# A cross-attention's query map folded into the context side, in a kernel of an RWKV block and an attention

## The chip, the cores and the metric

The kernel runs on one core of a Trainium2 chip. The metric is the device time of one execution in microseconds (us), and lower is better. The engines of the core run side by side and wait for each other by semaphores: TensorE (PE, matrix products into the PSUM memory), VectorE (DVE), ScalarE (ACT), GpSimd (POOL) and SyncE (SP), which here only issues DMAs. Work that one engine is given runs in the order in which it was put in that engine's queue.

## What is computed

Two layers run over 16 sequences of 128 tokens with 512 channels, in float32. The first is an RWKV block (layer norm, token mixing by small matrices, six large projections, a recurrence over time, a group norm and a feed-forward part). The second is a cross-attention between its result, `x_c`, and a context `x_s`. There the roles of the axes differ: the 128 tokens are the channels C, and the 512 channels are the positions T.

```python
def _inorm(x):                                   # over the last axis
    return (x - mean(x)) * rsqrt(var(x) + EPS)

Mn = einsum('oc,bct->bot', Wn, _inorm(x_c)) + bn     # queries
Mm = einsum('oc,bct->bot', Wm, _inorm(x_s)) + bm     # keys
A  = softmax(einsum('bct,bcs->bts', Mn, Mm), axis=-1)
Ml = einsum('oc,bct->bot', Wl, x_s) + bl             # values
Mo = einsum('bcs,bts->bct', Ml, A)
return einsum('oc,bct->bot', Wo, Mo) + bo + x_c
```

All of Wn, Wm, Wl and Wo are 128 x 128. For each of the 16 sequences the scores are a 512 x 512 matrix, and the softmax runs along its rows.

## The kernel before

The 16 sequences are worked in G = 8 groups of n = 2. Each group passes through stages, written as Python generators: `stageB` and `stageB2` (first norm, token mixing, projections), `stageR` (the recurrence), `stageC` (output projection, second norm, feed-forward part), `stageX` (loads the prepared context of the group) and `stageL` (the cross-attention, by `stageLb` for each of the two sequences). `stageE` prepares the contexts of all groups, by `context`, in the first three steps. In each step `interleave` takes pieces of the stages of different groups in turn, in an order given by `ORDER`, `DLY` and the numbers of pieces in `ST`; `NEED` says which stage of a group must be finished first. The framework's scheduler then fixes the order of every engine's queue before the run, and puts in the waits. Tiles come from pools: tiles with one tag share a fixed number of buffers, and a new tile waits until the old one of its slot is no longer read.

The weights' projections are plain matmuls: one float32 matmul is recorded as two passes on PE. All loads and stores are issued by SP, whose queue is in order too.

What the change touches:

- `load_late` (L86) loads the small constants, among them `bdm` (a mask of 128 x 8 x 16) and `emat` (a 0/1 matrix: partition p belongs to column p // 16), and the attention's weights in two loads, `wnm` (Wn and Wm) and `lo` (Wl and Wo). It multiplies Wl and Wo on PE once (`pc`), so that the values already carry the output map.
- `context` (L640) loads one context, normalises its rows (`inorm`, L635, on DVE, POOL and ACT), multiplies by Wm and adds bm on the way out of PSUM (`pm`, L649 and L650), makes the values (`pV`, L654 and L655) and writes both, 128 x 1024, to a DRAM tile `mvD` (L657). `stageX` loads it again as `MV`, just ahead of use (`MVl` for the last group).
- `stageLb` (L680) normalises the rows of x (`xh`), multiplies by Wn (`pn`, L687), adds bn on ACT (`Mn`, L689), and then works four tiles of 128 query positions. For each: scores `pS` (L693) on PE, the negated row maximum (L695) on DVE, exponential and row sum (L697) on ACT, reciprocal (L698) on DVE, scaling (L699) on ACT, four transposes into `pA` (L702) on PE and a copy to `AT` (L705) on ACT. After each two tiles the product with the values, `pO` (L711), is added to x (L713).
- In `stageR`, `spread` (L476) and the operation at L481 place states of the recurrence block by block into `Sx`, by a multiplication with `bdm`.

PSUM has eight banks, shared out by tags: `bx`, `c` and `lv` have two buffers each, `ls` and `la` one each. `pc`, `pm`, `pn` and `pS` use `ls`; `pV`, `pA` and `pO` use `la`. The last group takes others instead, where they are free by then. In SBUF the tag `e` has two buffers.

## Time and profile before

| | |
|---|---|
| runs, us | 993.84, 993.47, 990.04; median 993.47 |
| profiled execution, us | 989.27 |
| its span in the profile, us | 987.5 |
| busy PE, DVE, ACT, POOL, us | 903.8, 638.4, 502.4, 59.6 |
| mean clock granted to PE | 0.977 of full speed |

The profile is of one execution. The span runs from the first to the last instruction that it shows. Busy times are of the engines' instructions; as matmuls are pipelined, the recorded duration of a PE pass is longer than the time after which the next can follow. "PEld" are loads of the stationary operand of a matmul, which overlap with PE. Groups of instructions are listed with the line, engine and operation, the tile written, "<-" and the tiles read, their shape, the count, busy time in us and mean duration in ns, and after the bar the engine's idle time just before them, with what ended it. The chain of work that ended last is followed back from the last instruction, at each step to what released it. A number such as L687 is a line of the kernel before.

### The profile page before, as it was taken

How to read it: one execution, taken by the hardware profiler on the slowest of the kernel's cores; microseconds unless marked ns; L12 is line 12 of the kernel's file. 1: busy time of each engine (PE TensorE's matmuls, PEld its weight loads, DVE VectorE, ACT ScalarE, POOL GpSimd, SP SyncE). 2: the span in 40 equal slices, each digit the busy share in tenths (PEclk: the TensorE clock that was granted, in tenths of full speed). 3: DMA queues.
4: the chain of work that ended last, by engine and by line, in shares of the span. 5: the costliest groups of instructions: out<-in, count | busy, mean ns of one | idle time of the engine just before them, and what ended most of it. 6: DMA issues, size and time to landing. Idle time of an engine off the chain costs nothing.

```text
span 987.5 us, 19150 instructions
## 1 busy us (share of the span) xinstructions
PE 903.8 (92%) x7524; PEld 614.0 (62%) x7524; DVE 638.4 (65%) x1573; ACT 502.4 (51%) x1053; POOL 59.6 (6%) x92
## 2 busy tenths in 40 slices
PE   4889998899989999999999999999999979988966
PEld 3666767666745767486757676767657645654534
DVE  5786678945695849766877587846944587354131
ACT  4675273442464545644556456534552566367243
POOL 5120010001000100000001000000000000000000
PEclk9999999998999999999999999999999999999987
DMA  6575756355414444363436334543445322431300
GB/s 197 188 266 188 207 166 223 75 153 202 141 43 116 153 152 139 75 212 103 129 110 172 128 117 122 141 148 99 142 107 159 100 97 66 149 108 53 96 0 21
DMA packets 76603, 129.90 MB, mean 132 GB/s; under 512 B 33713, under 2 KB 43697, under 8 KB 76512
## 3 DMA queue, kind: packets, MB, share of 16 engines
q1 hardware_dynamic: 76514, 128.68, 42.4%
q8 instruction: 59, 0.97, 0.4%
q14 instruction: 30, 0.25, 0.1%
HBM read 100.32 MB, written 22.04 MB: 124 GB/s over the span
## 4 chain that ended last, share of the span: by engine, by line
PE 60%; DVE 19%; ACT 8%; DMA 6%; SPq 4%; issue 2%; POOL 1%; ACTq 0%; DVEq 0%; POOLq 0%
PE ptk L581 14%; PE pj L224 8%; PE pj L608 6%; PE pv L331 6%; PE pO L711 4%; PE pS L693 4%; PE pl L446 3%; DVE PP L384 3%; PE pA L702 2%; SPq L415 2%; DVE xm L289 2%; PE po L522 2%; DVE xm L290 1%; PE pa L515 1%; PE pu L494 1%
## 5 line engine op out<-in xcount | busy, mean ns | idle before, releaser
L224 PE MATMUL pj<-xm,wb 128*128 128x256 f32 x768 | 175.8, 381 | 2.1 <-DMA wb<-in_Wg_dram 1.4
L224 PEld LDWEIGHTS pj<-xm,wb 128*128 128x128 f32 x768 | 142.8, 190 | 27.2 <-issue 5.9
L143 POOL TENSOR_TENSOR rs<-rs,mhalf 128x1 f32<-128x1 f32 x64 | 41.5, 653 | 656.7 <-DVE rs L128 575.7
L693 PE MATMUL pS<-MV,Mn 128*128 128x512 f32 x112 | 59.8, 616 | 5.9 <-ACT e L697 5.2
L697 ACT ACTIVATE e<-pS,nm 128x512 f32<-128x512 f32 x64 | 44.4, 694 | 39.8 <-DVE nm L695 39.4
L695 DVE TENSOR_REDUCE nm<-pS 128x1 f32<-128x512 f32 x64 | 43.8, 687 | 30.4 <-PE pS L693 30.2
L608 PE MATMUL pj<-xk,wb 128*128 128x256 f32 x256 | 62.1, 396 | 0.2 <-DVE xk L150 0.2
L711 PE MATMUL pO<-AT,MV 128*128 128x256 f32 x224 | 58.4, 400 | 2.9 <-ACT AT L705 2.9
L331 PE MATMUL pv<-wb,xm 128*128 128x512 f32 x128 | 58.9, 610 | 1.4 <-DVE xm L289 1.4
L699 ACT ACTIVATE e<-e,nm 128x512 f32<-128x512 f32 x64 | 46.1, 725 | 27.1 <-DVE nm L698 27.0
L581 PE MATMUL ptk<-wb,sx 128*128 128x512 f32 x128 | 58.0, 597 | 1.4 <-ACT kk L611 1.4
L581 PE MATMUL ptk<-wb,kk 128*128 128x512 f32 x128 | 58.4, 596 | 0.2
L289 DVE TENSOR_TENSOR xm<-px,sx 128x512 f32<-128x512 f32 x80 | 53.6, 684 | 6.6 <-PE px L286 6.6
L581 PE MATMUL ptk<-wb,yT 128*128 128x512 f32 x128 | 57.2, 597 | 0.2
L608 PEld LDWEIGHTS pj<-xk,wb 128*128 128x128 f32 x256 | 49.9, 199 | 9.1 <-issue 1.0
L290 DVE TENSOR_TENSOR xm<-xm,xaT 128x512 f32<-128x512 f32 x80 | 54.3, 687 | 0.3
L702 PEld LDWEIGHTS pA<-ident,e 128*128 128x128 f32 x256 | 30.6, 143 | 35.1 <-issue 14.7
L713 DVE SCALAR_TENSOR_TENSOR x<-pO,cb,x 128x256 f32<-128x256 f32 x32 | 15.4, 480 | 55.9 <-PE pO L711 55.9
L702 PE MATMUL pA<-ident,e 128*128 128x128 f32 x256 | 41.1, 282 | 11.2 <-ACT e L699 7.5
L711 PEld LDWEIGHTS pO<-AT,MV 128*128 128x128 f32 x224 | 42.4, 196 | 14.0 <-issue 4.6
L705 ACT COPY AT<-pA 128x512 f32<-128x512 f32 x64 | 37.4, 584 | 24.0 <-PE pA L702 23.6
L286 PE MATMUL px<-sk,w2s 98*128 98x256 f32 x160 | 42.0, 357 | 7.7 <-DVE gt L345 2.7
(162 smaller groups left out, 1680.8 us busy)
## 6 DMA issues: line engine op xcount, KB each, us to landing
wb<-in_Wk_dram SPq DMA_DIRECT2D x16, 512.0 KB, 4.7
mvD<-MVe SPq DMA_DIRECT2D x16, 512.0 KB, 2.9
wb<-in_Wr_dram SPq DMA_DIRECT2D x16, 512.0 KB, 3.5
wb<-wvc SPq DMA_DIRECT2D x16, 512.0 KB, 3.4
wb<-in_Wg_dram SPq DMA_DIRECT2D x16, 512.0 KB, 3.5
wb<-in_Wo_dram SPq DMA_DIRECT2D x16, 512.0 KB, 3.6
wb<-in_Wfk_dram SPq DMA_DIRECT2D x16, 512.0 KB, 4.0
wb<-in_Wfr_dram SPq DMA_DIRECT2D x16, 512.0 KB, 3.9
```

What stands on the lines that cost most here:

```text
L224: nc.tensor.matmul(pj[:, m], lhsT=wb[:, m, cc, :], rhs=xm[:, cc], start=cc == 0, stop=cc == 3)
L289: nc.vector.tensor_tensor(xm[:, sl], px.rearrange("p c (b t) -> p c b t", b=n), sx[:, sl], ALU.mult)
L290: nc.vector.tensor_tensor(xm[:, sl], xm[:, sl], xaT[:, sl, :, 1:129], ALU.add)
L331: nc.tensor.matmul(pv, lhsT=xm[:, m, b], rhs=wbs[m // 2][:, m % 2], start=m == 0, stop=m == 3)
L581: nc.tensor.matmul(pt, lhsT=act[:, m, b], rhs=wbs[m // 2][:, m % 2], start=m == 0, stop=m == 3)
L608: nc.tensor.matmul(pj[:, m], lhsT=wb[:, m, cc, :], rhs=xk2[:, cc], start=cc == 0, stop=cc == 3)
L693: nc.tensor.matmul(pS, lhsT=Mn[:, tsl], rhs=Mm, start=True, stop=True)
L695: nc.vector.tensor_reduce(nm[:, 0:1], pS, AX.X, ALU.max, negate=True)
L697: nc.scalar.activation(e, pS, AF.Exp, bias=nm[:, 0:1], accum_out=nm[:, 1:2])
L699: nc.scalar.activation(e, e, AF.Identity, scale=nm[:, 2:3])
L702: nc.tensor.transpose(pA[:, sc], e[:, 128 * sc : 128 * sc + 128], ident)
L711: nc.tensor.matmul(pO, lhsT=Vc[:, sc], rhs=AT[:, sc], start=sc == 0, stop=sc == 3)
```

## The change

With h the normalised rows of x and g those of the context, the scores are (Wn h + bn)ᵀ(Wm g + bm). The part hᵀ Wnᵀ bm is kept with hᵀ(Wnᵀ Wm) g, and the parts that do not depend on h, bnᵀ Wm g + bnᵀ bm, form one bias for each column. So the change makes Wmᵀ Wn once in `load_late`, multiplies g by it in `context` instead of by Wm, with q0 = Wnᵀ bm as bias, and takes h itself as the stationary operand of the score matmul. `pn`, `Mn` and the map by Wn are gone from `stageLb`.

The column bias is made in `context` by a further matmul of four 32-column pieces, `pb`, which uses the `la` bank; ACT takes it to SBUF (`bt`, in the buffer of `AT`) with bnᵀ bm added, and it is written to a DRAM tile of 512 values, `btD`. `stageX` loads it, copied to all 128 partitions, as `BB` (`BBl` for the last group). In `stageLb` one DVE operation, `tensor_tensor_reduce`, adds the bias to the scores out of PSUM, negates, writes the result to `e` and gives its minimum along the row. The exponential then reads `e` instead of `pS`, with scale -1.

To make room in SBUF, `bdm` is dropped and `emat`, read with a broadcast innermost axis, takes its place, and `var`, `gv`, `gt` and `gr` have one buffer instead of two. The attention's weights come in one load. `xh` has two buffers instead of one.

```diff
-    td1, td2, l1b, emat, bdm, lvm, dgm = late.values()
-    wnm = const.tile([128, 2, 128], FP, name="wnm")
-    WnT, WmT = wnm[:, 0], wnm[:, 1]
+    td1, td2, l1b, emat, lvm, dgm = late.values()
+    wq = const.tile([128, 162], FP, name="wq")
+    wqT, q0, vk, kk0 = wq[:, 0:128], wq[:, 128:129], wq[:, 129:161], wq[:, 161:162]
...
-        nc.sync.dma_start(out=wnm, in_=a["l1w"][:, 0:2])
-        lo = sb.tile([128, 2, 128], FP, name="lo", tag="e", bufs=2)
-        nc.sync.dma_start(out=lo, in_=a["l1w"][:, 2:4])
-        Wl, WoT = lo[:, 0], lo[:, 1]
+        l1w = sb.tile([128, 4, 128], FP, name="l1w", tag="e", bufs=2)
+        nc.sync.dma_start(out=l1w, in_=a["l1w"])
+        Wn, Wm, Wl, WoT = (l1w[:, i, :] for i in range(4))
...
+        bnr = sb.tile([128, 128], FP, name="bnr", tag="e", bufs=2)
+        nc.vector.tensor_scalar(bnr, ident, 0.0, l1b[:, 0:1], ALU.mult, ALU.add)
+        pq = pc[:, 129:291]
+        nc.tensor.matmul(pq[:, 0:128], lhsT=Wm, rhs=Wn, start=True, stop=True)
+        nc.tensor.matmul(pq[:, 128:129], lhsT=Wn, rhs=l1b[:, 1:2], start=True, stop=True)
+        nc.tensor.matmul(pq[:, 129:161], lhsT=Wm, rhs=bnr[:, 0:32], start=True, stop=True)
+        nc.tensor.matmul(pq[:, 161:162], lhsT=bnr, rhs=l1b[:, 1:2], start=True, stop=True)
+        nc.vector.tensor_copy(wq, pq)
...
-        var = small.tile([128, n, 32], FP, name="var", bufs=2)
+        var = small.tile([128, n, 32], FP, name="var", bufs=1)
...
-                o = Sx[:, c].rearrange("p m (a q) j -> p m a (q j)", a=2)
-                nc.vector.tensor_tensor(o, src, bdm.rearrange("p (a q) j -> p a (q j)", a=2)[:, None].to_broadcast([128, 4, 2, 64]), ALU.mult)
+                o = Sx[:, c].rearrange("p m (a q) j -> p m a q j", a=2)
+                own = emat[:, 0:8].rearrange("p (a q) -> p a q", a=2)[:, None, :, :, None].to_broadcast([128, 4, 2, 4, 16])
+                nc.vector.tensor_tensor(o, src, own, ALU.mult)
...
-    def inorm(xap, tag, how, ssum=None, tile_=dict(tag="l1n", bufs=1)):
+    def inorm(xap, tag, how, ssum=None, tile_=dict(tag="l1n", bufs=2)):
...
+        pb = ps.tile([128, 128], FP, name="pb", **T("la"))
+        for sc in range(4):
+            nc.tensor.matmul(pb[32 * sc : 32 * sc + 32], lhsT=vk, rhs=xsn[:, 128 * sc : 128 * sc + 128], start=True, stop=True)
+        bt = sb1.tile([128, 128], FP, name="bt", tag="AT")
+        nc.scalar.activation(bt, pb, AF.Identity, bias=kk0)
+        btD = dr.tile([1, 512], FP, name="btD", bufs=16)
+        nc.sync.dma_start(out=btD.rearrange("o (c s) -> (o c) s", c=4), in_=bt[0:128:32])
         pm = ps.tile([128, 512], FP, name="pm", **T("ls"))
-        nc.tensor.matmul(pm, lhsT=WmT, rhs=xsn, start=True, stop=True)
-        nc.scalar.activation(mv[:, 0:512], pm, AF.Identity, bias=l1b[:, 1:2])
+        nc.tensor.matmul(pm, lhsT=wqT, rhs=xsn, start=True, stop=True)
+        nc.scalar.activation(mv[:, 0:512], pm, AF.Identity, bias=q0)
...
             with behind(g + 2):
-                nc.sync.dma_start(out=mv, in_=d["mvD"][b])
-            d["MV"].append(mv)
+                nc.sync.dma_start(out=mv, in_=d["mvD"][b][0])
+                nc.sync.dma_start(out=bb, in_=d["mvD"][b][1].to_broadcast([128, 512]))
+            d["MV"].append((mv, bb))
...
         xh = inorm(xb, "xh", "act", d["ssum"][b])
-        pn = ps.tile([128, 512], FP, name="pn", **T("ls", g, ("lv", "bx")[b]))
-        nc.tensor.matmul(pn, lhsT=WnT, rhs=xh, start=True, stop=True)
-        Mn = sb.tile([128, 512], FP, name="Mn")
-        nc.scalar.activation(Mn, pn, AF.Identity, bias=l1b[:, 0:1])
         for tt in range(4):
             tsl = slice(128 * tt, 128 * tt + 128)
             pS = ps.tile([128, 512], FP, name="pS", **T("ls", g, ("c", "lv")[b]))
-            nc.tensor.matmul(pS, lhsT=Mn[:, tsl], rhs=Mm, start=True, stop=True)
+            nc.tensor.matmul(pS, lhsT=xh[:, tsl], rhs=Qm, start=True, stop=True)
             nm = small.tile([128, 3], FP, name="nm")
-            nc.vector.tensor_reduce(nm[:, 0:1], pS, AX.X, ALU.max, negate=True)
             e = sb.tile([128, 512], FP, name="e")
-            nc.scalar.activation(e, pS, AF.Exp, bias=nm[:, 0:1], accum_out=nm[:, 1:2])
+
+            nc.vector.tensor_tensor_reduce(e, pS, bb, -1.0, 3.4e38, ALU.add, ALU.min, nm[:, 0:1])
+            nc.scalar.activation(e, e, AF.Exp, bias=nm[:, 0:1], scale=-1.0, accum_out=nm[:, 1:2])
```

`WnT` and the like are transposed on the host before, and `Wn` and `Wm` are passed as they are after. The load of `bdm` and its preparation on the host are gone as well.

## The prediction

> **What bounds the kernel now.** I read the page's busy shares first, then its slices, then busy time by stage, because a share over the whole span mixes stages with different limits.
>
> ```profile
> PE 903.8 (92%) x7524; PEld 614.0 (62%) x7524; DVE 638.4 (65%) x1573; ACT 502.4 (51%) x1053; POOL 59.6 (6%) x92
> ...
> PEclk9999999998999999999999999999999999999987
> ```
>
> TensorE (PE) is busy for 92% of the span at an almost full clock; ScalarE (ACT) for half. By stage (stretch, PE, weight loads, VectorE (DVE), ACT, GpSimd, clock, DMA):
>
> ```profile
> 15.00:143.00 128.00, 116.93 (x868) 85.69 (x869) 97.73 (x274) 74.77 (x158) 19.09 (x27) 0.99 0.63 204
> ...
> 400.00:700.00 300.00, 297.64 (x2660) 208.00 (x2659) 210.58 (x504) 158.58 (x342) 10.01 (x20) 1.00 0.44 133
> ...
> 880.00:988.00 108.00, 81.31 (x354) 47.40 (x351) 31.86 (x86) 48.49 (x96) 2.19 (x4) 0.88 0.12 39
> ```
>
> From 400 to 700 us PE idles 2.4 us in 300: matmul time removed there is time gained. Up to 143 us, where the contexts are prepared, PE idles 9%, and in the last 108 us 25% (the last groups' attention, one step after another). The chain of work that ended last agrees: PE 60%, DVE 19%. The groups of the attention, by shape (line, engine, operation, count, busy us, mean ns, idle before and its releaser):
>
> ```profile
> L687 PE MATMUL pn<-l1n,wnm 128*128 128x512 f32 x32 | 18.1, 650 | 8.4 <-ACT e L697 5.0 <-ACT l1n L145 3.4
> L689 ACT ACTIVATE Mn<-pn,l1b 128x512 f32<-128x512 f32 x16 | 11.0, 687 | 6.9 <-PE pn L687 6.8
> L693 PE MATMUL pS<-MV,Mn 128*128 128x512 f32 x112 | 59.8, 616 | 5.9 <-ACT e L697 5.2 <-ACT Mn L689 0.6
> L695 DVE TENSOR_REDUCE nm<-pS 128x1 f32<-128x512 f32 x64 | 43.8, 687 | 30.4 <-PE pS L693 30.2
> L697 ACT ACTIVATE e<-pS,nm 128x512 f32<-128x512 f32 x64 | 44.4, 694 | 39.8 <-DVE nm L695 39.4
> ```
>
> The query map is 16 float32 matmuls in 32 passes; before them PE idles 8.4 us, mostly until an exponential frees the one-buffer "ls" bank. A mean of 650 ns is no price, since passes overlap. The chain lists 16 passes of the same width (ptk) in 7.07 us: 0.44 us each.
>
> **The change part by part.**
>
> Query map gone. 32 x 0.43 us (6.87 us for 16 in an undisturbed piece of the chain) = -13.7 us of PE. 16 bias activations of 0.687 us = -11.0 us of ACT, which does not set the pace; they count only in the tail, below.
>
> "ls" freed earlier. The bank is now released by DVE, not by the exponential after it (0.69 us and its queue). Idle for that reason: 5.0 us at pn, 5.2 us at pS. Bounds: 0 (the static order finds another wait) and -10.2; I take -4, since in 400 to 700 us only 0.2 us of such a wait was seen, and elsewhere PE often meets another wait next (xh, the normalised rows, 3.4 us at pn now).
>
> Tail. The last group's first score tile waits today from 944.39 (pn starts) to 946.29 (pS starts): pn 1.14, Mn 0.70. The other half has pn on the chain for 1.71. Sum 3.6, of which 1.7 (four passes) is already counted: -1.9.
>
> Per-context bias (stage E), PE. pb is four 128x32 matmuls in four column groups, 8 passes. L446 has exactly this shape: 64 passes in 1.89 us, 0.03 each, since four groups run side by side. 16 x 8 x 0.03 = +3.8. If they did not share the array, pV's price holds (8 passes in 1.16 us, 0.145): +18.6. I take 3.8, the identical shape.
>
> Per-context bias, waits. pb takes the one-buffer "la" bank that only pV used here. pV needs just xs and today often runs while xs is normalised (at 21.52, before pm at 22.52); it must now share the bank with pb, which needs the normalised rows and an ACT evacuation (128x128 out of PSUM: L303, 0.284). Queued behind a waiting pV on PE: the projections; behind pV's end: the next xs load, on the SP queue (it waits for pV 7.3 us in all today). Bounds: 0 where PE finds the bank free, and about 1.6 us per context (pb 0.24, bt 0.28, and one ACT queue of the kind seen at 24.74, where pV's copy stood behind 4 us of casts) = +26. I take 0.25 us per context, +4, near the evacuation alone, because today's pV idles PE 3.2 us over 16 contexts (L654), 0.2 each, on the same bank. bt lies in the single AT buffer until its write has been read out (the mvD writes land in 2.9 us); 16 contexts in 118 us come some 7 us apart: 0, and where two come close ACT waits up to 2.9 us, with mv's copies behind it.
>
> DVE's fused operation. 64 reductions of 0.687 are replaced by 64 operations that also read bb and write e. Nearest rows: scalar_tensor_tensor with an accumulator, one input in PSUM (L586, 689 ns + an 83 ns read, which overlaps its end) and two float32 SBUF inputs (L628, 690 + 83). So +0.09 x 64 = +5.5 us of DVE at most; at DVE's 19% of the chain, +1. Bounds from both sides: 0, and 1.22 us each (y<-y,gr, L546: twice the elements, as if two cycles per element), +34 us of DVE. I take the accumulator rows: same streams, same count of elements. **A page against it:** the Trainium skill, Vector Engine (DVE) Microarchitecture Reference, "Points that are easy to get wrong", says a scalar_tensor_tensor with two non-bf16 SBUF sources runs at half throughput. L628 is just that and takes 690 ns, against 689 with PSUM as one source, so the trace does not show the halving; by the rule, were it to hold here, the term would be the +34 above rather than +5.5.
>
> e is written by DVE instead of ACT, so DVE now waits for e's slot (two buffers: the transposes of two tiles before). Queued behind it on DVE: the recurrence's PP, AM and Sx, and PE waits for those. Between 400 and 700 us a group has 8 tiles in 105 us (the chain shows y, L546, at 491.72 and 596.95), some 13 us each, against about 4 us from maximum to transposes: 0; in the tail, where tiles follow faster, DVE has nothing else to do. Bounds 0 and +5.
>
> Exponential out of SBUF instead of PSUM: L699 (725) against L697 (694): 64 x 0.03 = +2 of ACT, hidden by its idle half; 0.1 in the tail.
>
> Masks. Sx by emat broadcast instead of bdm: 64 operations, same elements. Broadcast innermost operands cost nothing today (L502: 128x256 in 420 ns, as L503 without in 415): 0. The single-buffered var, gv, gt, gr are written and read by DVE alone, in order: 0. l1n with two buffers: a wait fewer, 0.
>
> DMA. 16 writes of bt (2 KB) and 16 loads of bb (256 KB, of the 512 KB kind that land in 3.5 us), each 0.33 us of SP issue: +10.6 us of SP. Past them on SP go KX, VX, weights and s0. The SP queue is 4% of the chain: 10.6 x 0.04 = 0.4; with the write waiting for bt ahead of mvD I take +1 (bounds 0 and 10.6). Two loads fewer at the start, one on the starting chain (13.79, 0.43): -0.4.
>
> Once: Wm·Wn, q0, vk, kk0 on PE, priced like pc (0.80 + 0.38): 0.8 + 3 x 0.4 = 2 us near 20 us, while PE idles half; the l1w and bnr tiles hold both "e" slots that the first contexts need: +1 (bounds 0 and 3).
>
> Sum: -13.7 - 4 - 1.9 + 3.8 + 4 + 1 + 1 - 0.4 + 1 = **-9.2 us**. The profiled execution took 989.27 us (span 987.5), the runs' median is 993.47, with 990.04 the lowest: the profiled one is shorter than each of them. Its time would become 980; the median 984, which I predict.
>
> **The rivals.** What counts as a change: 0.5%, or 5 us (988.5 to 998.4), about what a measurement of this kernel can tell.
>
> A, the sum above: PE's saved passes are paid out, 984 (972 to 988). For it: 400 to 700 us at 99% PE, in which three of eight groups' maps fall.
>
> B, paid out only where PE has no slack. Three of eight groups lie in 400 to 700: -5.1; in 143 to 400 and from 700 to 880 another wait takes over (PE idles 6 to 9% there), the tail's 1.9 stays, and the +7.8 of stage E and the +2.6 of the rest are due: +3.4, 997, no change. Against it: the chain runs through pn at 396 and 944 too, outside that stretch.
>
> C, slower: stage E's bank. It decides once a context costs 0.9 us more than the 0.25 taken: -9.2 + 14.4 = +5. At 1.5 us, near the queue bound, -9.2 + 20 = +11: 1004. For it: mvD, xs, pm and pV are all on the chain before 100 us, and PE's order is static. Against it: the extra evacuation is only 0.28 us.
>
> D, the fused operation at 1.22 us. 34 us of DVE; 4 of the 64 lie in the tail's chain (+2.1), the rest at a third on the path (+10.6): +12.7 instead of +1, 996. Against it: L586.
>
> **How the numbers follow.** A 0.60, B 0.18, C 0.15, D 0.07. D's 996 is inside the 5 us, but half of it lies above, and static orders can also fall badly in A. So faster 0.60, same 0.18, slower 0.22. Low end: both PE waits gone (-10.2 for -4) and stage E free of waits (0 for +4), -19.4, and 2 more for a luckier order: 972. High end: just under C's 1004, 1002; below 972 and above 1002 lie about 2 in 10.
>
> **What the profile after would show.** pn and Mn absent; PE busy near 894 us; pS waiting on DVE instead of ACT; pb's 128 passes with hardly any chain share; the fused operation at 0.69 to 0.78 us; the stretch from 15 to 143 us as long as now, within 8 us. The prediction is wrong if the contexts end well after 143 us, if the fused operation takes over 1 us, or if PE's idle time between 400 and 700 grows by more than 5 us.

## The result and the profile after

The changed kernel takes 996.06 us (median of 20 executions, 993.02 to 999.41), the kernel before beside it on the same chip 991.76 us (20 executions, 987.44 to 996.91). The ratio is 1.0044, with a 95% interval of 1.0027 to 1.0060. The change makes the kernel slower by 0.4%, which is inside the 0.5% that the prediction called no change; forecast was a gain of 1%, with a chance of 0.60 for faster.

The profiled execution of the changed kernel took 996.0 us, its span 994.2. Its page gives, as busy shares and as the row of TensorE's clock:

```profile
PE 905.9 (91%) x7628; PEld 613.7 (62%) x7628; DVE 639.0 (64%) x1639; ACT 496.3 (50%) x1053; POOL 58.0 (6%) x92
...
PEclk9889999999999999999999999999999999999887
```

The passes are those expected: 7524 - 32 + 128 + 8 = 7628. By stage (stretch, PE, weight loads, DVE, ACT, POOL, clock, DMA share, GB/s):

```profile
15.00:143.00 128.00, 111.79 (x898) 81.13 (x898) 92.49 (x251) 66.13 (x150) 16.31 (x22) 0.95 0.53 172
...
400.00:700.00 300.00, 298.21 (x2670) 204.14 (x2669) 212.21 (x537) 158.46 (x348) 10.94 (x20) 1.00 0.46 141
...
880.00:995.00 115.00, 84.31 (x376) 49.62 (x376) 37.78 (x119) 51.99 (x104) 2.74 (x5) 0.89 0.13 43
```

From 400 to 700 us PE is as busy as before. Up to 143 us it is busy 111.79 us where it was 116.93. That is the start, where the contexts are prepared, and there they end later. This is the copy of the values out of PSUM, the last thing that a context does on ACT, first in the kernel before and then in the changed one (durations min/median/max in ns, then the first and last start in us):

```profile
L655 ACT COPY MVe<-pV x16: 563/586/589, 23.5 to 138.1; 128x512 f32<-128x512 f32 x16
```

```profile
L672 ACT COPY MVe<-pV x16: 564/585/674, 31.2 to 205.4; 128x512 f32<-128x512 f32 x16
```

The last context is done at 205.4 us and not at 138.1. The groups of the attention on the page after, and two of VectorE's and one of SP's waits over the whole span (us in all, times, longest):

```profile
L709 PE MATMUL pS<-MV,l1n 128*128 128x512 f32 x112 | 59.3, 611 | 7.3 <-DVE nm L713 5.2
...
L714 ACT ACTIVATE e<-e,nm 128x512 f32<-128x512 f32 x64 | 46.4, 725 | 35.2 <-DVE nm L713 34.5
...
L713 DVE CUSTOM_DVE_ANT_0 e<-pS,BB 128x512 f32<-128x512 f32 x56 | 38.4, 685 | 18.0 <-PE pS L709 11.9
```

```profile
DVE e L713 <- PE pS L709: 16.1, 16, 4.2
DVE e L713 <- PE pA L719: 8.2, 5, 4.0
```

```profile
SPq L664 <- ACT bt L662: 29.0, 10, 8.6
```

The values' wait for the bank "la" in the start (10 to 190 us before, 10 to 210 after), first in the kernel before and then in the changed one:

```profile
PE pV L654 <- ACT MVe L655: 2.4, 3, 1.0
```

```profile
PE pV L671 <- ACT bt L662: 4.1, 3, 2.8
```

pn and Mn are gone; the fused operation takes 685 ns. pS now waits for DVE, 5.2 us, what it waited for ACT before; the 5.0 us that pn waited for the same bank are gone with pn. DVE has a wait that the kernel before had not: 8.2 us until the transposes pA have read an older e. SP's queue stands 29.0 us in front of the store of the bias row.

Two measures of my own are used below. Both are estimates. **TensorE's work**: each pass is given the time after which the next one follows in an undisturbed piece (0.43 us for a pass of 128 by 512, 0.03 for one of pb), and these are added over all passes. It is 843.8 us before and 834.6 after, 9.2 less; what is left of the time to the end of the trace's last pass is **idle time**, 140 us before and 156 after. **The y multiplies**: one DVE operation at the end of each group's recurrence, eight in a run, which divide it into a start, seven steps and a tail.

| us | before | after |
|---|---|---|
| start, to the first y multiply | 187.8 | 196.3 |
| idle in it | 42.6 | 52.6 |
| the seven steps together | 703.6 | 703.1 |
| idle in them | 63.5 | 64.5 |
| tail | 92.6 | 91.2 |
| idle in it | 34.0 | 38.7 |

So the passes saved did not come out anywhere. In the start 10 us of idle time came in; in the tail PE had 6.1 us less to do and was idle 4.7 us longer; the steps stayed as long as they were. But the y multiplies mark dates and not equal pieces of work, and with a new order of the queues other work moves across them. Of the map's 32 passes 28 started within the steps, 12 us of work, and yet the steps hold only 1.5 us of work less (640.1 to 638.6 us). The second y multiply comes at 288.8 us, which is ahead of the 292.2 before. So between two orders it is the idle time that tells where time went.

### The profile page after: what moved, and what is told of

Same layout as the page of the kernel before. It is cut to its first block, busy times and chain, and to the rows that moved or that the text cites. A ratio compares the mean times of both kernels' runs of the same rounds, so it can differ in the third digit from the quotient of the medians.

```text
span 994.2 us, 19466 instructions
## 1 busy us (share of the span) xinstructions
PE 905.9 (91%) x7628; PEld 613.7 (62%) x7628; DVE 639.0 (64%) x1639; ACT 496.3 (50%) x1053; POOL 58.0 (6%) x92
## 4 chain that ended last, share of the span: by engine, by line
PE 60%; DVE 19%; ACT 8%; DMA 6%; SPq 3%; issue 2%; POOL 0%; DVEq 0%; ACTq 0%; POOLq 0%
PE ptk L590 13%; PE pj L232 9%; PE pj L617 6%; PE pv L339 5%; PE pO L728 5%; PE pS L709 4%; PE pl L454 4%; DVE PP L392 3%; PE pA L719 2%; SPq L423 2%; PE p L253 2%; DVE xm L297 1%; DVE xm L298 1%; DMA xs<-in_ctx_dram 1%; PE po L531 1%
## 5 line engine op out<-in xcount | busy, mean ns | idle before, releaser
L232 PE MATMUL pj<-xm,wb 128*128 128x256 f32 x768 | 180.5, 383 | 2.7 <-DVE xm L297 1.4
L151 POOL TENSOR_TENSOR rs<-rs,mhalf 128x1 f32<-128x1 f32 x64 | 42.7, 672 | 753.4 <-DVE rs L136 560.8
L709 PE MATMUL pS<-MV,l1n 128*128 128x512 f32 x112 | 59.3, 611 | 7.3 <-DVE nm L713 5.2
L714 ACT ACTIVATE e<-e,nm 128x512 f32<-128x512 f32 x64 | 46.4, 725 | 35.2 <-DVE nm L713 34.5
L590 PE MATMUL ptk<-wb,sx 128*128 128x512 f32 x128 | 60.2, 613 | 3.4 <-DMA wb<-in_Wfr_dram 3.4
L728 PE MATMUL pO<-AT,MV 128*128 128x256 f32 x224 | 54.7, 386 | 5.4 <-ACT AT L722 5.4
L617 PEld LDWEIGHTS pj<-xk,wb 128*128 128x128 f32 x256 | 49.2, 198 | 11.3 <-issue 4.3
L716 ACT ACTIVATE e<-e,nm 128x512 f32<-128x512 f32 x64 | 45.7, 720 | 13.9 <-DVE nm L715 13.6
L719 PE MATMUL pA<-ident,e 128*128 128x128 f32 x256 | 41.5, 284 | 10.6 <-ACT AT L722 5.5
L713 DVE CUSTOM_DVE_ANT_0 e<-pS,BB 128x512 f32<-128x512 f32 x56 | 38.4, 685 | 18.0 <-PE pS L709 11.9
L454 PE MATMUL pl<-KX,r 128*32 128x128 f32 x1536 | 48.6, 274 | 1.1 <-DVE AM L410 1.1
L454 PEld LDWEIGHTS pl<-KX,r 128*32 128x32 f32 x1536 | 40.8, 110 | 13.1 <-issue 11.1
```

The lines of the kernel that those rows point to most:

```text
L232: nc.tensor.matmul(pj[:, m], lhsT=wb[:, m, cc, :], rhs=xm[:, cc], start=cc == 0, stop=cc == 3)
L454: nc.tensor.matmul(t[cs, 128 * cc : 128 * cc + 128], lhsT=r[:, cc, b, cs], rhs=KX[:, n * cc + b, :, 16 * c : 16 * c + 16], start=True, sto ...
L590: nc.tensor.matmul(pt, lhsT=act[:, m, b], rhs=wbs[m // 2][:, m % 2], start=m == 0, stop=m == 3)
L617: nc.tensor.matmul(pj[:, m], lhsT=wb[:, m, cc, :], rhs=xk2[:, cc], start=cc == 0, stop=cc == 3)
L709: nc.tensor.matmul(pS, lhsT=xh[:, tsl], rhs=Qm, start=True, stop=True)
L714: nc.scalar.activation(e, e, AF.Exp, bias=nm[:, 0:1], scale=-1.0, accum_out=nm[:, 1:2])
```

## The experiments

### Does the work removed pay by itself?

Each "Measured" below is the ratio to the time of the kernel before, run beside it, with its 95% interval.

The first four runs took the change apart, by the theory of the prediction: removed passes pay where PE is full, and stage E takes back some.

**e1_nomap**, the kernel before without the query map (which is left out of what is computed):

```diff
-    def inorm(xap, tag, how, ssum=None, tile_=dict(tag="l1n", bufs=1)):
+    def inorm(xap, tag, how, ssum=None, tile_=dict(tag="l1n", bufs=2)):
...
-        pn = ps.tile([128, 512], FP, name="pn", **T("ls", g, ("lv", "bx")[b]))
-        nc.tensor.matmul(pn, lhsT=WnT, rhs=xh, start=True, stop=True)
-        Mn = sb.tile([128, 512], FP, name="Mn")
-        nc.scalar.activation(Mn, pn, AF.Identity, bias=l1b[:, 0:1])
...
-            nc.tensor.matmul(pS, lhsT=Mn[:, tsl], rhs=Mm, start=True, stop=True)
+            nc.tensor.matmul(pS, lhsT=xh[:, tsl], rhs=Mm, start=True, stop=True)
```

> The kernel before with the query map left out: pn and Mn are gone, the scores are taken from the normalised rows and the keys as they are, and xh has two buffers; nothing is added, so bn and Wn are missing from the output. It measures the saving alone. Theory S (stage E gives the gain back): the 32 passes at 0.43 us are paid out, and the tail's wait too, so 12 to 16 us below the kernel before, ratio 0.984 to 0.988. Theory M (the middle doesn't pay: with less work PE's queue comes in smaller pieces, and each switch of shape costs 0.1 to 0.2 us): 2 to 7 us below, ratio 0.993 to 0.998, with the distance of two y operations in the middle of the run still near 105 us.

Measured: 1.0169 (1.0131 to 1.0208). Taking 13.7 us of passes out, and adding nothing, made the kernel 1.7% slower.

**e2_nobias**, the changed kernel without the bias part (left out of what is computed):

```diff
+    bb0 = const.tile([128, 512], FP, name="bb0")
+    nc.gpsimd.memset(bb0, 0.0)
...
-        pb = ps.tile([128, 128], FP, name="pb", **T("la"))
-        for sc in range(4):
-            nc.tensor.matmul(pb[32 * sc : 32 * sc + 32], lhsT=vk, rhs=xsn[:, 128 * sc : 128 * sc + 128], start=True, stop=True)
-        bt = sb1.tile([128, 128], FP, name="bt", tag="AT")
-        nc.scalar.activation(bt, pb, AF.Identity, bias=kk0)
...
-            d["MV"].append((mv, bb))
+            d["MV"].append((mv, bb0))
```

> The changed kernel without the column bias: pb, bt, their store and the 16 loads of BB are gone, and the fused DVE operation adds a constant tile of zeros; the bias bn meets the keys nowhere. All else stays. Theory S: the contexts end near 140 us again instead of 205, and the time falls by 12 to 18 us against the changed kernel, to a ratio of 0.985 to 0.992 against before. Theory M: the contexts end early too, but the run ends within 5 us of the changed kernel, ratio 0.999 to 1.009. If it lies more than 3 us above the kernel without the map, the fused operation costs that.

Measured: 1.0238 (1.0194 to 1.0281). Without the bias part the contexts end at 141.8 us, as before, and the kernel is slower than with it.

**e3_pvfirst**, the changed kernel with the values ahead of pb in the bank "la", and the store of bt behind that of mv:

```diff
+        pV = ps.tile([128, 512], FP, name="pV", **T("la"))
+        for sc in range(4):
+            sl = slice(128 * sc, 128 * sc + 128)
+            nc.tensor.matmul(pV[:, sl], lhsT=xs[:, sl], rhs=wcT, start=True, stop=True)
+        nc.scalar.copy(mv[:, 512:1024], pV)
         pb = ps.tile([128, 128], FP, name="pb", **T("la"))
...
         nc.sync.dma_start(out=mvD, in_=mv)
+        nc.sync.dma_start(out=btD.rearrange("o (c s) -> (o c) s", c=4), in_=bt[0:128:32])
```

> The changed kernel with two moves in the preparation of a context: the values pV are made ahead of pb, as they need only the raw rows, and the store of bt is issued behind the store of mv instead of ahead of it. Output as before. Theory S, with the one la bank and the SP queue as the cause: xs is free as early as in the kernel before, SP no longer waits 29 us for bt, the contexts end before 170 us, and the time falls 4 to 10 us against the changed kernel, ratio 0.994 to 1.000. If the cause is the bias chain's length in itself or PE's order in the middle: within 2 us of the changed kernel, ratio 1.002 to 1.006.

Measured: 1.0161 (1.0121 to 1.0200). The contexts end at 195.8 us. This is slower than the changed kernel and outside both ranges that were expected.

**e4_house**, the kernel before with the changed kernel's small savings of memory (`emat` for `bdm`, one buffer for `var`, `gv`, `gt` and `gr`):

```diff
-        var = small.tile([128, n, 32], FP, name="var", bufs=2)
+        var = small.tile([128, n, 32], FP, name="var", bufs=1)
...
-                                    bdm[:, None].to_broadcast([128, 4, 8, 16]), ALU.mult)
+                                    emat[:, None, 0:8, None].to_broadcast([128, 4, 8, 16]), ALU.mult)
```

> The kernel before with only the housekeeping of the change: the masks of Sx from emat with a broadcast innermost axis instead of bdm, and one buffer for var, gv, gt and gr. The prediction priced both at nothing: ratio 0.998 to 1.002, Sx at 0.69 us. If single buffers or the broadcast cost something, or if the queues' order alone moves the time, 3 us or more either way.

Measured: 1.0026 (1.0005 to 1.0047), within 0.5%. By the interval they cost a little, about 2.6 us, but they are not what makes e1_nomap and e2_nobias slow.

e1_nomap and e2_nobias both lose in the middle. Between the second and the fifth y multiply e1_nomap has steps with 9.1, 9.3 and 7.2 us of idle time, e2_nobias 11.7, 16.5 and 11.8, where the kernel before had 2.7, 4.8 and 3.5. Neither the bias part nor its place in stage E can be what does that. Two explanations were left: the framework's scheduler lays out all five queues anew for every source, and the new order is worse; or something in the data's dependences changed.

### The same work in the order of the kernel before

To separate them I held the order. At the end of the kernel's function, every instruction that has a counterpart in the kernel before is chained, per engine, to the one that precedes it there, with a dependence that orders but needs no semaphore. What has no counterpart is still placed by the scheduler.

```diff
+    for row in order.split(";"):
+        name, at = row.split(":")
+        at = [engine[name][int(k)] for k in at.split()]
+        for p, q in zip(at, at[1:]):
+            tc.add_manual_dep(q, p.name, mybir.DependencyInfo(mybir.DependencyClass.NoSync, mybir.DependencyReason.DATA),
+                              reason="issue order")
```

**f1_nomap_order** is e1_nomap with this order.

> The kernel of e1_nomap (the kernel before without pn and Mn; the query map is left out of what is computed), in which every instruction that the kernel before also has is held to that kernel's order on its own engine: 4178 of TensorE, 1541 of VectorE, 940 of ScalarE, 534 transfers of SP, 88 of GpSimd. Nothing else differs from e1_nomap, which ran 1.0169 times as long as the kernel before. Theory O (the order: taking work out made the program's planner lay out all five queues anew, and the new layout waits more): the passes removed, 32 by 428 ns = 13.7 us less of TensorE's work, are now paid out: 973 us beside 987 of before on the same chip (ratio 0.986, 0.980 to 0.992). Theory W (the work removed was never what TensorE had to wait for: the middle of the kernel is bound by chains through ScalarE, VectorE and the transfers, so that idle time takes the place of the passes in any order): no faster than before, ratio 0.996 to 1.005. Theory S (what went wrong in e1_nomap is the second l1n buffer or the missing step between the normalised row and the scores): ratio 1.010 to 1.020 as in e1_nomap.

Measured: 1.0132 (1.0099 to 1.0166). The theory that the order alone is at fault fell: with the order of before, 16 matmuls and 16 activations fewer still cost 1.3%. But now the two traces can be laid side by side, instruction by instruction. ScalarE's waits from 200 to 900 us have a line that the kernel before has not:

```profile
ACT l1n L142 <- PE pS L690: 22.5, 3, 7.9
```

L142 is the Square of the row norm, which writes into xh's tile. In the kernel before that tile was read once, by pn, and its result lay in Mn, with two buffers more. Now the four score matmuls read xh itself, so its buffer comes free only at the last of them. The chain from the norm to the scores had three buffers (one l1n, two Mn); it has two. ScalarE stands up to 7.9 us, and the keys ks of the recurrence, which are behind it in its queue, come late for their transfer to KX (SP's queue from 400 to 700 us, where the kernel before has 5.5 us for the same wait):

```profile
SPq L416 <- ACT ks L412: 19.4, 3, 12.2
```

In the same stretch PE waits

```profile
PE pA L699 <- DVE x L710: 5.1, 2, 2.5
PE pq L396 <- DVE PP L385: 5.0, 3, 2.4
```

where the kernel before has 1.2 us for PP and no wait of pA for x. The way from ScalarE's wait to these two is argued from the order of the queues; what shows that the buffer matters is the third buffer, below.

**f2_after_order** is the changed kernel in the order of before. For such an order to exist, pb had to leave "la" for "ls" behind pm, and the small tile mj (L192) needed a buffer of its own:

```diff
-            mj = sb1.tile([128, 64], FP, name="mj", tag="AT")
+            mj = sb1.tile([128, 64], FP, name="mj")
...
-        pb = ps.tile([128, 128], FP, name="pb", **T("la"))
+        pb = ps.tile([128, 128], FP, name="pb", **T("ls"))
```

> The changed kernel, in which every instruction that the kernel before also has is held to that kernel's order on its own engine (the fused operations stand in the places of the maxima, but for the last six). Two things had to be moved for such an order to exist: pb's bank is ls in place of la, behind pm, and the small tile mj of the start has a buffer of its own. All is computed. Theory O: the sum of the prediction is now paid out, -9.2 of TensorE's time, with up to 10 us lost again in stage E where bt and pb stand in the chain: 978 us beside 987 of before (ratio 0.991, 0.985 to 1.002), and below g1_after_free by at least 0.8%. Theory W: ratio 1.000 to 1.008, as the changed kernel and g1_after_free. If the fused operation itself is the trouble (it writes e, so the maximum of one tile waits for the buffer of e, and the exponential waits 800 ns and not 600 ns), ratio 1.003 to 1.010 here while f1_nomap_order is under 0.992.

Measured: 1.0463 (1.0432 to 1.0494), far slower than anything expected.

**f3_nobias_order** is e2_nobias in the order of before.

> The kernel of e2_nobias (the changed kernel without pb, bt, btD and BB; the fused operation adds a constant tile of zeros, so the bias part is left out of what is computed), held to the order of the kernel before on every engine. Free of that order it ran 1.0238 times as long as the kernel before. Theory O: -12.8 us of TensorE's time (843.8 to 831.0 us of passes), paid out: 975 us, ratio 0.988 (0.982 to 0.996); the difference to f1_nomap_order is the price of the fused operation against the maximum alone (64 instructions, 95 ns each longer), within 0.4%, and the difference to f2_after_order is that of the bias part's computation. Theory W: 0.998 to 1.006.

Measured: 1.0259 (1.0231 to 1.0287), above both ranges as well, and no better than e2_nobias in the scheduler's order.

**g1_after_free** is the source of f2_after_order with the order left to the scheduler.

> The control to f2_after_order: the same source (the changed kernel with pb in ls behind pm, and mj in its own buffer), its order left to the planner. Theory O: another of the layouts that the planner happens on, 1.000 to 1.025 as the four others that were tried (1.0026 to 1.0238), and slower than f2_after_order by at least 0.8%. Theory W: within 0.4% of f2_after_order.

Measured: 1.0051 (1.0024 to 1.0079). It has the time of the changed kernel, although its contexts end at 169.9 us and not at 205.4: that date by itself does not set the time.

### A third buffer for xh

**f4_nomap_order_l3** changes one number of f1_nomap_order, **e5_nomap_l3** the same number of e1_nomap, **e6_nobias_l3** that of e2_nobias:

```diff
-    def inorm(xap, tag, how, ssum=None, tile_=dict(tag="l1n", bufs=2)):
+    def inorm(xap, tag, how, ssum=None, tile_=dict(tag="l1n", bufs=3)):
```

> f1_nomap_order (the kernel before without pn and Mn, in the order of the kernel before on every engine; the query map is left out of what is computed) with one number changed: three l1n buffers in place of two. Theory L (the life of xh: with pn gone the four score matmuls of a row block read xh itself, so its buffer comes free at the last of them and not at pn; the kernel before had one l1n and two Mn tiles, three in the chain, and f1_nomap_order has two. ScalarE's next Square stands and waits for the buffer, 22.5 us in 3 waits between 200 and 900 us, 7.9 the longest, and the keys ks, their transfer to KX and PP are late behind it): that wait falls below 3 us, the steps between the y multiplies from 400 to 720 us fall from 110 to 112 us back to 104, and the time is 973 us beside 987 of before (ratio 0.986, 0.980 to 0.993). Theory W (in the middle of the kernel TensorE is not what the passes are waiting for, so passes removed become idle time however many buffers there are): ratio 1.000 to 1.014.

Measured: 0.9934 (0.9905 to 0.9963), from 1.0132. ScalarE's wait on pS is gone from its list, and SP's for the keys is down from 19.4 us:

```profile
SPq L416 <- ACT ks L412: 7.2, 2, 3.6
```

The stretch from 400 to 700 us, first of f1_nomap_order, then of f4_nomap_order_l3:

```profile
400.00:700.00 300.00, 287.96 (x2500) 197.37 (x2501) 203.67 (x487) 150.71 (x327) 10.04 (x20) 0.98 0.41 126
```

```profile
400.00:700.00 300.00, 295.52 (x2657) 207.07 (x2656) 210.82 (x505) 155.28 (x336) 10.02 (x20) 1.00 0.43 133
```

157 passes more fit into the same 300 us. The steps there fall from 110.3 and 112.1 us to 105.2 and 104.7. In one and the same order, the buffer is worth 2.0%. Not all of that has to be waiting: the clock granted to PE in this stretch was 0.98 with two buffers and 1.00 with three, and 2% of 300 us is 6 us of a full engine's time. How much comes by the clock was not separated. Of PE's two waits above, only that of pA for x is gone; pq waits 5.0 us for PP between 200 and 900 us in both runs. The Trainium skill, Perfetto Trace Analysis, "Optimization Strategy", says that a gap which repeats on the engine that should be full can mean too few buffers for the next tile. Here that holds, but the waits of PE name other tiles (x and PP): the missing buffer is seen in ScalarE's waits.

> e1_nomap (without pn and Mn; the query map is left out of what is computed; order left to the planner; ratio 1.0169) with three l1n buffers in place of two. Theory L: 0.984 to 0.998, the idle time between the second and the fifth y multiply back from 8.5 us in each step to 4. A theory that the planner's order is at fault beside the buffers: 1.000 to 1.015 while f4_nomap_order_l3 is under 0.993. Theory W: both 1.000 to 1.015.

Measured: 1.0116 (1.0078 to 1.0153). This is exactly the work and the buffers of f4_nomap_order_l3; only the order differs, and it costs 1.8%. So the order counts as well. SP's wait for the keys between 200 and 900 us, first of e5_nomap_l3, then of f4_nomap_order_l3:

```profile
SPq L415 <- ACT ks L411: 68.3, 5, 17.2
```

```profile
SPq L416 <- ACT ks L412: 29.5, 5, 12.1
```

With two buffers the two causes had hidden each other: the scheduler's order for e1_nomap has only one wait of 2.2 us for xh's buffer, but keeps SP's queue 69.8 us behind the keys, against 42.7 us in f1_nomap_order. In the scheduler's order the third buffer gave 0.5% (1.0169 to 1.0116), which the intervals do not clear of nothing.

> e2_nobias (the changed kernel without pb, bt, btD and BB, with a constant tile of zeros in the fused operation, so that the bias part is left out of what is computed; ratio 1.0238) with three l1n buffers in place of two. Theory L: 0.986 to 1.000. The theory that the fused operation itself makes the middle slow (it writes e, and so waits for a buffer of e where the maximum alone did not): 1.015 to 1.025, as e2_nobias. Theory W: 1.000 to 1.014.

Measured: 1.0221 (1.0193 to 1.0248), as e2_nobias. In the scheduler's order the third buffer alone does nothing here, and e2_nobias shows no wait for xh's buffer: why it is slow in that order stays open.

**h2_after_ls_l3** is g1_after_free with the third buffer; the bias row goes to bfloat16 to make the room. All is computed.

```diff
-        bt = sb1.tile([128, 128], FP, name="bt", tag="AT")
+        bt = sb1.tile([128, 128], BF, name="bt", tag="AT")
...
-                bb = sb.tile([128, 512], FP, name="BB")
+                bb = sb.tile([128, 512], BF, name="BB")
```

> g1_after_free (the changed kernel with pb in ls behind pm and mj in its own buffer; ratio 1.0051) with three l1n buffers in place of two; the room for the third comes from keeping the bias row (bt, btD, BB) in bfloat16. All is computed. In g1_after_free the middle was already at 104.7 to 105.4 us a step and its loss lay in the start (first y multiply with 48.7 us of idle TensorE time, 42.6 before) and the tail (40.0, 34.9 before). Theory L: the middle gains 1 us a step at most, so 0.994 to 1.002; if the buffers hold up stage L of the changed kernel more than its waits show, 0.985 to 0.994. Theory W: 1.002 to 1.010.

Measured: 1.0056 (1.0033 to 1.0079), as g1_after_free: with everything computed, the third buffer and the bfloat16 row brought nothing in the scheduler's order.

### The fused operation and the bias part, in the order of before

**j2_nobias_order_l3** is f3_nobias_order with the third buffer.

> f3_nobias_order (the changed kernel without the bias part, which is left out of what is computed, a tile of zeros in its place; order of the kernel before; ratio 1.0259) with three l1n buffers in place of two. If the buffer of xh is all: 0.993, as f4_nomap_order_l3. If the fused operation's wait for a buffer of e counts beside it (9.0 us the longest wait of VectorE behind pA in f3_nobias_order): 1.000 to 1.015.

Measured: 1.0083 (1.0051 to 1.0116), from 1.0259: the buffer is worth 1.8% here. DVE's waits from 400 to 700 us show what else there is:

```profile
DVE e L706 <- PE pS L702: 11.2, 6, 3.8
DVE e L706 <- PE pA L712: 10.8, 2, 9.0
```

The second line is the wait for a buffer of e: the fused operation writes e, where the maximum wrote only one column. DVE's queue stands for up to 9.0 us.

**j3_nobias_order_ps** lets the fused operation write its sum back over the scores in PSUM:

```diff
-            nc.vector.tensor_tensor_reduce(e, pS, bb, -1.0, 3.4e38, ALU.add, ALU.min, nm[:, 0:1])
-            nc.scalar.activation(e, e, AF.Exp, bias=nm[:, 0:1], scale=-1.0, accum_out=nm[:, 1:2])
+            nc.vector.tensor_tensor_reduce(pS, pS, bb, -1.0, 3.4e38, ALU.add, ALU.min, nm[:, 0:1])
+            nc.scalar.activation(e, pS, AF.Exp, bias=nm[:, 0:1], scale=-1.0, accum_out=nm[:, 1:2])
```

> j2_nobias_order_l3 with the fused operation writing over pS in place of e, and the exponential reading pS; the bias part is left out as there. 0.993 to 0.997 if the write to e was what remained; as j2 if it was not; 0.3% to 0.8% above f4_nomap_order_l3 if the fused operation's own length (95 ns more than the maximum, 64 times, on the way from pS to the exponential) counts.

Measured: 1.0024 (1.0001 to 1.0047). The six last fused operations are now held to the order too, which they were not in j2_nobias_order_l3. The write to e cost 0.6%, and the wait is gone; the bank "ls" is held until the exponential again, as in the kernel before. Against f4_nomap_order_l3 there remains 0.9%, more than expected. The two differ by the fused operation in place of the maximum, the products made once at the start, the tile of zeros, and the small savings of memory, which took 0.26% by themselves in e4_house; which of them takes how much was not separated.

**j1_after_order_ps** is the changed kernel with the three remedies, in the order of before, and with pb, bt, btD and BB given places in that order.

> The changed kernel with everything computed, in the order of the kernel before on every engine, with four things mended: three l1n buffers (room from a bias row in bfloat16); the fused operation writes its sum back over pS in PSUM and the exponential reads it there, so that e is written no earlier than before; pb, bt and btD have places of their own in the order (pb eight steps of TensorE behind pm, bt two steps behind the copy of pm, btD behind the store of mvD); mj in its own buffer. If the three causes (the buffer of xh, the wait for e, the bias part standing badly in stage E) are what made f2_after_order 1.0463: 0.993 + 4.5 us of pb and pq = 0.998, range 0.993 to 1.006. If the bias part costs stage E more wherever it stands (ScalarE has 16 more activations and SP 16 more stores to put between): 1.006 to 1.025. If the order of before can't be kept by other work without loss: over 1.025.

Measured: 1.0224 (1.0197 to 1.0252). Its steps from 412.7 to 834.0 us are 106.0, 105.0, 105.1 and 105.2 us, those of f4_nomap_order_l3 to within some tenths until the last; most of the loss lies in the start. (This execution, 1016.41 us, is the longest of its six, whose median is 1010.28; its tail is 6.0 us longer than that of j3_nobias_order_ps.) The y multiplies of j3_nobias_order_ps and then of j1_after_order_ps (first and last start):

```profile
L558 DVE TENSOR_TENSOR y<-y,gr x8: 1208/1224/1226, 190.5 to 893.4; 128x1024 f32<-128x1024 f32 x8
```

```profile
L557 DVE TENSOR_TENSOR y<-y,gr x8: 1209/1225/1226, 213.6 to 914.1; 128x1024 f32<-128x1024 f32 x8
```

The bias part costs 23.1 us before the first y multiply. Waits of PE and ACT there, from 15 to 165 us, that j3_nobias_order_ps has not:

```profile
PE pm L661 <- ACT bt L667: 11.0, 8, 6.8
```

```profile
ACT l1n L155 <- PE pb L665: 11.2, 5, 3.0
ACT bt L667 <- DMA btD<-bt: 5.6, 2, 4.2
```

**k1_bias_from_q** takes pb away and leaves the 16 activations, stores and loads where they were (the bias values are then not those wanted):

```diff
-        pb = ps.tile([128, 128], FP, name="pb", **T("ls"))
-        for sc in range(4):
-            nc.tensor.matmul(pb[32 * sc : 32 * sc + 32], lhsT=vk, rhs=xsn[:, 128 * sc : 128 * sc + 128], start=True, stop=True)
...
-        nc.scalar.activation(bt, pb, AF.Identity, bias=kk0)
+        nc.scalar.activation(bt, mv[:, 0:128], AF.Identity, bias=kk0)
```

> j1_after_order_ps without the 64 matmuls pb: bt is computed from the first 128 columns of the copy of pm in SBUF, so that ScalarE's 16 activations, the 16 stores btD and the loads BB stay where they stood, and the bank of pm and the normalised context are held no longer than in the kernel before. The values of the bias part are not those wanted; that is what is left out. If pb's hold of the bank and of the normalised context is the cost (in j1_after_order_ps pm waits 11.0 us for bt, and ScalarE's normalising step 11.2 us for pb, both before 165 us): the first y multiply at 190 to 195 us, ratio 1.000 to 1.006. If the activations and transfers in the queues are: the first y multiply at 207 to 214, ratio 1.015 to 1.023.

Measured: 1.0132 (1.0086 to 1.0179), with the first y multiply at 202.3 us: between the two expectations. Half of the 23.1 us (11.3) is pb, with its passes, its bank and its hold of the normalised context, and half (11.8) what is left of the bias part, the activations and transfers in the queues of ACT and SP. These dates are of one execution each; the ratios of all executions split alike, 0.9% for pb (1.0224 to 1.0132) and 1.1% for the rest (1.0132 to 1.0024). How the second half is shared between ACT and SP was not separated.

### A version that is faster than both

**g3_after_free_ps** is the source of j1_after_order_ps with the order left to the scheduler: the changed kernel, everything computed, with three buffers for xh, a bfloat16 bias row, pb in "ls" and the fused operation writing to PSUM.

> The source of j1_after_order_ps with no order held: the planner lays it out. All is computed. If the planner's layout is worth a per cent or two either way, as e5_nomap_l3 against f4_nomap_order_l3 (1.0116 against 0.9934): 1.004 to 1.025, and slower than j1_after_order_ps. If the wait for e was what the free layouts lost: 0.992 to 1.000.

Measured: 984.05 us beside 987.71 of the kernel before, ratio 0.9959 (0.9942 to 0.9976). Against h2_after_ls_l3 the source differs only by where the fused operation writes, and the ratio by 1.0%. Over its whole span h2_after_ls_l3 has a wait of DVE that g3_after_free_ps has not:

```profile
DVE e L714 <- PE pA L720: 22.1, 8, 4.6
```

In g3_after_free_ps the first y multiply comes at 176.9 us, against 187.8 in the kernel before, but the next at 299.4, against 292.2, so the early date is no gain in itself; the steps between 399.4 and 711.6 us are 104.3, 104.3 and 103.6 us, and only the last y multiply is ahead again (884.5 against 891.4). It is not shown how much of the 1.0% is the wait for e and how much the new order.

**k2_after_free_c** puts pb into the banks "c", right behind pm and ahead of pm's copy:

```diff
-        nc.scalar.activation(mv[:, 0:512], pm, AF.Identity, bias=q0)
-        pb = ps.tile([128, 128], FP, name="pb", **T("ls"))
+        pb = ps.tile([128, 128], FP, name="pb", **T("c"))
...
+        nc.scalar.activation(mv[:, 0:512], pm, AF.Identity, bias=q0)
```

> g3_after_free_ps (all computed, order left to the planner, 0.9959) with pb in the two banks c, right behind pm, in place of ls. If pb's hold of pm's bank costs the start something there too: 0.988 to 0.995. If the layout decides: anything from 0.993 to 1.015, with the start's first y multiply not earlier than 176.9 us.

Measured: 1.0191 (1.0149 to 1.0234). It has the same work as g3_after_free_ps, pb's banks and the place of pm's copy in the source apart, and is 2.3% slower; its steps between 404.9 and 734.5 us are 126.4, 106.4 and 96.8, far from the contexts. The likely reading is that the order decides, and what pb's bank is worth stays hidden under it; as the order was not held here, that is not shown.

## Why the prediction was wrong

The terms of PE's work were close: 843.8 to 834.6 us is -9.2, beside -13.7 of the map, +3.8 of pb and about +1 for the products made once (-8.9). What failed is the step from work to time: that removed passes are paid out where PE is 99% busy, and that a tile held longer costs nothing.

- **"Query map gone ... -13.7"**, on the ground that "matmul time removed there is time gained". In the best case measured (f4_nomap_order_l3: same order, buffers enough) 0.66% of 989 us came out, 6.5 us, between 3.7 and 9.4 by the interval. The rest became idle time in small pieces that I cannot put down to one wait. In the scheduler's own order the same removal costs 1.7% (e1_nomap). A PE busy for 297 of 300 us does not show that its passes set the pace. The three steps from the third to the sixth y multiply take 316.0 us in f4_nomap_order_l3, in the order of before, and 315.9 in the kernel before, though 12 of the map's passes (5.2 us) are missing from them; in these two executions the gain comes behind them, mostly in the next step (102.7 us for 108.7). The Trainium skill (Perfetto Trace Analysis, "Identifying the Most-Contended Engine") says that the busy share of matmuls is no good measure of how near TensorE is to its limit, because pipelined instructions look smaller in the trace. This case agrees on the measure, with 298.21 of 300 us busy in steps that hold 5 us of idle time each by the undisturbed pitch of the passes. It does not agree on the reason: a score pass is recorded as longer than its pitch (611 ns on average, against 430), not as smaller.
- **"l1n with two buffers: a wait fewer, 0"** is the step that failed most clearly where the order is held. I counted the new buffer and not the longer hold: four score matmuls instead of one pn, and two Mn buffers gone. It is worth 2.0% (f1 against f4) and 1.8% (f3 against j2) in a held order. I had even written that xh's rows are what PE meets next, and did not follow it to ScalarE. In the changed kernel itself the scheduler laid its order around this (ACT waits 0.3 us for that reason), and a third buffer did not help in its orders (g1_after_free to h2_after_ls_l3, e2_nobias to e6_nobias_l3). If the shortage has a price there, it is in the order, and that is not shown.
- **"ls freed earlier ... -4"** brought no time. pS waits 5.2 us for DVE now where it waited 5.2 for ACT; pn's 5.0 us went with pn. In a held order, the write to e that frees the bank early costs 0.6% with the wait for e that it brings (j2 against j3); the earlier release alone was not measured.
- **"e is written by DVE ... 0", bounds 0 and +5.** The wait is in the changed kernel (8.2 us) and in j2 (10.8 us of 300). My reasoning, 13 us between tiles against 4 us from maximum to transposes, was a mean; in the kernel before the seven score tiles from 441 to 525 us start between 6 and 26 us apart.
- **"Per-context bias, waits ... +4".** In the changed kernel the start has 10 us of idle time more. The bank "la" is not where it went: pV waits 4.1 us for bt there, where it waited 2.4 us for its own copy before (bt took 367 ns, against the 284 of the row taken for it). In the order of before the bias part puts the first y multiply 23.1 us later; without pb's own 3.8 that is 19.3 us of waits in one execution, within the bound of 26 and just past the 18.4 (4 + 14.4) from which rival C decides. Half of the 23.1 lies with pb, which there shares "ls" and not "la"; the other half is in ACT's and SP's queues, and the DMA term for SP's was +1, left open up to 10.6.
- **"Tail -1.9"**: 92.6 to 91.2 us, -1.4, near in number. But PE's work in the tail fell by 6.1 us, of which the map's four passes are 1.7 and the rest is work that moved forward, and most of it became idle time; so the number is not a confirmation.
- **"DVE's fused operation +1", 0.69 to 0.78 us**: 685 ns, and the read of its result 83 ns; the duration was right and rival D out. (The rule of the Trainium skill weighed there, Vector Engine (DVE) Microarchitecture Reference, "Points that are easy to get wrong", is of two SBUF sources; here one source is PSUM, and no run has the fused operation with two.) The 0.9% of j3 against f4, in which it is one of four differences, is more than the 2 us that the sum had for it and for the products made once.
- **Masks and single buffers, 0**: e4_house is at 1.0026 (1.0005 to 1.0047): small, but not nothing, in an order that the scheduler laid anew.
- **"Start" and "Once"**: the first y multiply of j3_nobias_order_ps is 2.9 us later than that of f4_nomap_order_l3, at the upper bound of 3.

Of the signs named, pS waiting on DVE and the fused operation's time held. "PE busy near 894" did not: 905.9, and records of busy time turned out too coarse for a few us of work. "The contexts end well after 143 us" was named as what would prove the prediction wrong, and it is what happened; the other two were not seen (the fused operation at 0.69 us, PE's idle time between 400 and 700 us 1.8 us after 2.4 by busy time). Yet g1_after_free and e2_nobias show that this date does not set the time. Rival B's time, 997, is near the result, but by another mechanism: it let the passes pay from 400 to 700 us, just where f4_nomap_order_l3 shows that they do not.

What remains open: what makes up the changed kernel's own 0.4%, as no edit in the scheduler's order took away one cause and left the order alone; which of the scheduler's choices make one order 1.8% better than another for the same work (e5 against f4), why half of the removed passes did not pay in f4, and what makes up the 0.9% of j3 against f4.

## What to carry to other kernels

Before removing a copy, count it as a buffer: ask which tile is now read longer, how many buffers the chain has left, and which in-order queue will stand in front of that tile. When a scheduler fixes the queues' order, an edit is compared with the old kernel only if the order is held; here the same work in two orders differed by 1.8%, more than the whole change could give. And here the work removed from a full engine, 13.7 us, was an upper bound of the gain, not the gain.

## What the runs showed of the hardware

The fused operation that adds a 128 by 512 tile in SBUF to one in PSUM and gives the row minimum takes 685 ns, as long as a maximum alone over the same tile (687 ns), plus 83 ns to read the result. Written back to PSUM it takes 699 ns and 141 ns (j3_nobias_order_ps). So reading a second stream and writing a full tile cost DVE next to nothing in duration; what they cost came through the buffers.

The clock granted to PE between 15 and 143 us was 0.99 before, 0.95 after and 0.91 in j1_after_order_ps, in the order in which PE was busy there: 116.93, 111.79 and 109.84 us. Whether the lower clock follows from the gaps or adds to them is not shown.
